# Moving denominators and a unit's last values up to the next unit's first logits in an attention kernel

## The chip, the cores and the metric

The kernel runs on one core of a Trainium2 chip. The metric is the device time of one execution in microseconds; the time before is the median of three runs, and a separate execution was taken by the hardware profiler. Engines are named as in the profile: PE is TensorE's matmul stream and PEld its weight loads, DVE is VectorE, ACT is ScalarE, POOL is GpSimd, SP is SyncE, whose queue issues the transfers.

## What is computed

Eight images of 512 channels by 32x32 pixels, all in float32, go through two layers. The part that matters here is the attention in the first layer, which is run twice for each image (`i` = 0, 1):

```python
def bot_attention(x, qkv_w, rw, rh):
    b, c, h, w = x.shape
    hw = h * w
    qkv = conv2d(x, qkv_w, 0).reshape(b, 3, HEADS, HD, hw)
    q, k, v = (qkv[:, 0], qkv[:, 1], qkv[:, 2])
    r = (rw + rh).reshape(1, HEADS, HD, hw)
    logits = jnp.einsum('bhdi,bhdj->bhij', q, k + r) * HD ** (-0.5)
    a = jax.nn.softmax(logits, axis=-1)
    out = jnp.einsum('bhij,bhdj->bhdi', a, v)
    return out.reshape(b, c, h, w)
...
t = cbs(x, cv1_w, cv1_bn, 0)
ys = [t[:, :C], t[:, C:]]
for i in range(N):
    yi = ys[-1]
    z = cbs(yi, m_cv1_w[i], m_cv1_bn[i], 1)
    z = bot_attention(z, m_qkv_w[i], m_rw[i], m_rh[i])
    z = jax.nn.silu(bn_eval(conv2d(z, m_cv2_w[i], 0), m_cv2_bn[i]))
    ys.append(yi + z)
return cbs(jnp.concatenate(ys, axis=1), cv2_w, cv2_bn, 0)
```

There are 4 heads of 64 channels (`HD`) over 1024 pixels. `cbs` is a convolution, a batch norm with fixed statistics and a silu; `cv1`, `cv2` and `m_cv2` are 1x1 convolutions and `m_cv1` is 3x3. A group norm precedes each layer, and the second layer is a 1x1 convolution with a masked weight. Both layers are added to their input.

## The kernel before

The attention is cut into 64 units. A unit is one image, one `i`, one pair of heads (`hp`) and one half of the 1024 queries (512 columns). Four units make a slot (one image and `i`), and there are 16 slots. The logits are kept transposed: keys lie on the partitions, in eight tiles (`KT` = 8), and queries lie along the columns.

The steps of a unit, with their lines and the names that the profile shows:

- `logits(t)` (L502, `lg`): one matmul for each of the two heads, on 64 rows of the array each, into a bank of PSUM each. ScalarE copies both to SBUF (L508, `st`), and VectorE keeps the running maximum over the tiles (L513, `mx`).
- `top` (L521, L522): TensorE transposes the maxima (`mt`, eight transposes in two banks), and VectorE reduces each bank to the negated maximum of each query (`nm`).
- `spread` (L529, `mb`): eight more transposes bring the negated maxima back along the columns.
- `soften(t)` (L533): VectorE adds `mb` to the logits of a tile; `exponent(t)` (L537) takes the exponent on ScalarE, and GpSimd adds the result to a running sum (L542, `sum`; `acc` in the code).
- `values(t)` (L548, `po`): two matmuls, one for each head, on 64 columns of the array each, accumulate the eight tiles in one PSUM tile `po`.
- `finish` (L560, L562): two matmuls with ones give the denominators (`den`), also on 64 columns each, and ScalarE copies them to `rb`. `divide(part)` (L567, L569) takes the reciprocal of half of `rb` and multiplies that half of `po` by it into `q`, on VectorE.

All other work of TensorE is filler between the units' steps: the 1x1 convolutions (L175: `cv`, `qk`, `l`, `m`), the 3x3 convolution in a transformed form (L305, `m`) and the products of `v` (L397). `slot_filler` lists it for each slot. `advance(share)` takes filler from this list until the given share of the slot is reached; `steps` is 40, ten for each unit, and `base` is ten times the unit's number in its slot. `Clock` keeps a planned time: `tick` moves it on and issues what has become due, such as the statistics of a group norm.

The order in the loop is written out by hand, and a scheduler may still exchange instructions that are close together. While unit `u` does its softmax, the logits of the next unit `nxt` are issued among its steps, two tiles at a time. `before` is the unit ahead of `u`. So around a change of unit the order before is: last logits of `u`, filler, `values(6)` and `values(7)` of `before`, transposes `mt` of `u`, filler, `mb`, filler, `den` of `before`, and then in the loop at t = 0 the softening of `u` and the first two logits of `nxt`.

`in_turn` and `act_turn` fix the order of the named VectorE and ScalarE instructions among themselves. The pools that matter: five PSUM banks (`ps_f`) shared by `lg`, `mt`, `den` and all filler; one buffer each for `mb` (two banks) and `po`; ten buffers `st`, of which a unit fills eight; one buffer each for `mx` and `acc`.

Of the kernel before, what the change touches and what calls it, by code (L numbers as in the profile page):

```python
# [32 lines left out]
KT = 8  # L33
# [6 lines left out]
def conv_preact_kernel(ctx: ExitStack, tc: tile.TileContext, x, cv1, cv2, mcv1, qkv, mcv2, bn, rw, rh, conv, s_in, t_in, out):  # L40
# [27 lines left out]
    def bank(name):  # L68
        return ps_f.tile([P, HALF], F32, tag="bank", name=name)

    def half_tile(name):
        return tp.tile([P, HALF], F32, tag="t", name=name)
# [413 lines left out]
    class Unit:  # L486
# [69 lines left out]
        def finish(self):  # L556

            den = bank(f"den_{self.name}")
            for h in range(2):
                nc.tensor.matmul(den[HD * h : HD * h + HD], ones[:, :HD], self.acc[:, h], start=True, stop=True)  # L560
            self.rb = half_tile(f"rb_{self.name}")
            nc.scalar.copy(self.rb, den)  # L562
            self.divide(0)

        def divide(self, part):
            r = ts(part, HALF // 2)
# [184 lines left out]
    clock = Clock()  # L751
# [140 lines left out]
    def slot_filler(s):  # L892

        prev = slots[s - 1] if s else (None, 0)
        nxt = slots[s + 1] if s + 1 < len(slots) else (None, 0)
        todo, needed = [], 0.0

        def add(us, g):
            nonlocal needed
            todo.append((us, g))  # L900
            needed += us

        im, i = nxt
        add(8.0, bg.take(8.0))
        if im and i == 1:
            add(7.0, im.conv_m2(0))
            add(0.0, call(im.transform, 1, 3.0, 1.0))
            add(9.0, bg.take(9.0))
        products = im.conv3(i) if im else iter(())
        if prev[1] == 1:  # L910
            if im:
                add(21.3, (us for _, us in zip(range(16), products)))
            add(7.0, prev[0].conv_m2(1))
            add(0.0, call(lambda: finishing(prev[0])))
        if im:
            add(10.7 if prev[1] == 1 else 32.0, products)
            add(7.0, bg.take(7.0))
        if im:
            add(21.0, im.project(i))
        if s + 2 < len(slots) and slots[s + 2][1] == 0:  # L920
            add(0.0, call(slots[s + 2][0].load_y))
            add(0.0, call(slots[s + 2][0].transform, 0, 8.0, 1.3))
        rest = SHARE - needed if im else 70.0
        if rest > 0:
            todo.append((rest, bg.take(rest, wait=True)))
        total = sum(c for c, _ in todo)
        return needed, total, todo
# [76 lines left out]
    before = None  # L1004
    for s in range(len(slots)):
        needed, total, todo = slot_filler(s)
        state = {"done": 0.0}

        def filler():
            for us, g in todo:  # L1010
                start = state["done"]
                for cost in g:
                    clock.tick(cost)
                    state["done"] += cost
                    yield

                state["done"] = max(state["done"], start + us)

        fill = filler()

        def advance(share):
            goal = max(share * total, min(1.0, share / 0.74) * needed + 0.1)
            while state["done"] < goal:
                if next(fill, "end") == "end":
                    break

        steps = 4 * (KT + 2)
        for j in range(4):
            u = units[4 * s + j]
            nxt = units[4 * s + j + 1] if 4 * s + j + 1 < len(units) else None  # L1030
            base = j * (KT + 2)
            u.top()
            clock.tick(0.9)
            advance((base + 1) / steps)
            u.spread()
            clock.tick(0.9)
            advance((base + 2) / steps)
            if before:
                before.finish()
                clock.tick(0.9)  # L1040
            for t in range(0, KT, 2):
                u.soften(t)
                if before and t == 0:
                    before.divide(1)
                u.soften(t + 1)
                if t:
                    u.exponent(t)
                    u.values(t - 2)
                    u.values(t - 1)
                    clock.tick(2.0)  # L1050
                if nxt:
                    nxt.logits(t)
                    nxt.logits(t + 1)
                    clock.tick(2.0)

                if not t:
                    u.exponent(t)
                u.exponent(t + 1)
                advance((base + 4 + t) / steps)
            u.values(KT - 2)  # L1060
            u.values(KT - 1)
            clock.tick(2.0)
            before = u
        for _ in fill:
            pass

    before.finish()
    before.divide(1)
    im = images[NB - 1]
    clock.run(bg.take(7.0, force=True))  # L1070
# [54 lines left out]
```

## Time and profile before

| what | value |
|---|---|
| median of the runs | 3250.11 us (3249.44 to 3253.17, three runs) |
| profiled execution, its own time | 3244.98 us |
| span of the profiled execution | 3243.3 us |
| granted TensorE clock | 0.994 |
| PE busy | 3141.8 us, 11668 records |
| DVE busy | 2071.7 us |
| ACT busy | 1727.1 us |
| POOL busy | 1243.3 us |
| DMA | 399.28 MB, mean 123 GB/s |

The span is from the first to the last instruction. Busy is the time in which at least one instruction of the engine was shown running; the ends of matmuls are modelled, so that a matmul's length in the list can reach into the next one, and the distance from start to start says how long the array was taken. A float32 matmul leaves two records, a transpose one. A wait in the lists is idle time of an engine just before an instruction, put down to what ended it last.

### The profile page before, as it was taken

How to read it: one execution, taken by the hardware profiler on the slowest of the kernel's cores; microseconds unless marked ns; L12 is line 12 of the kernel's file. 1: busy time of each engine (PE TensorE's matmuls, PEld its weight loads, DVE VectorE, ACT ScalarE, POOL GpSimd, SP SyncE). 2: the span in 40 equal slices, each digit the busy share in tenths (PEclk: the TensorE clock that was granted, in tenths of full speed). 3: DMA queues.
4: the chain of work that ended last, by engine and by line, in shares of the span. 5: the costliest groups of instructions: out<-in, count | busy, mean ns of one | idle time of the engine just before them, and what ended most of it. 6: DMA issues, size and time to landing. Idle time of an engine off the chain costs nothing.

```text
span 3243.3 us, 33195 instructions
## 1 busy us (share of the span) xinstructions
PE 3141.8 (97%) x11668; PEld 1519.6 (47%) x11668; DVE 2071.7 (64%) x2718; ACT 1727.1 (53%) x2353; POOL 1243.3 (38%) x971
## 2 busy tenths in 40 slices
PE   7999999999999999999999999999999999999999
PEld 3645444454445454454445454454445454453343
DVE  5446676667666576667666676667666676666642
ACT  3255765854655555544655455554645455555631
POOL 2113343445433444344434443345434443344420
PEclk9999999999999999999999999999999999999999
DMA  8841442421233232423233242423233241413366
GB/s 295 301 158 62 158 151 81 142 79 59 88 113 127 69 133 69 143 85 136 88 111 130 89 138 67 145 81 132 95 111 123 88 146 58 154 62 120 104 213 218
DMA packets 142006, 399.28 MB, mean 123 GB/s; under 512 B 13072, under 2 KB 14352, under 8 KB 141840
## 3 DMA queue, kind: packets, MB, share of 16 engines
q1 hardware_dynamic: 141120, 396.94, 36.4%
q8 instruction: 92, 1.51, 0.2%
q14 instruction: 74, 0.61, 0.1%
q10 hardware_dynamic: 720, 0.23, 0.0%
HBM read 317.42 MB, written 79.69 MB: 122 GB/s over the span
## 4 chain that ended last, share of the span: by engine, by line
PE 72%; DVE 11%; ACT 5%; DMA 4%; issue 3%; POOL 0%; SPq 0%; ACTq 0%; DVEq 0%
PE cv L175 14%; PE m L305 14%; PE po L548 12%; PE lg L502 11%; PE qk L175 6%; PE l L175 5%; PE v L397 3%; DVE st L533 2%; DVE rb L567 2%; PE mt L521 2%; PE den L560 2%; PE mb L529 2%; DVE mx L513 2%; PE m L175 1%; DMA x<-in_x 1%
## 5 line engine op out<-in xcount | busy, mean ns | idle before, releaser
L542 POOL TENSOR_TENSOR sum<-sum,st 128x512 f32<-128x512 f32 x768 | 993.8, 1319 | 719.2 <-ACT st L537 719.1
L537 ACT ACTIVATE st<-st 128x1024 f32<-128x1024 f32 x512 | 540.8, 1069 | 390.9 <-DVE st L533 389.8
L513 DVE TENSOR_TENSOR mx<-mx,lg 128x512 f32<-128x512 f32 x768 | 477.6, 682 | 370.2 <-ACT st L508 370.1
L533 DVE TENSOR_TENSOR st<-st,mb 128x1024 f32<-128x1024 f32 x512 | 604.9, 1214 | 71.3 <-PE mb L529 71.3
L508 ACT COPY st<-lg 128x512 f32<-128x512 f32 x1024 | 524.4, 596 | 228.0 <-PE lg L502 222.8
L305 PE MATMUL m<-plane,w_m 128*128 128x256 f32 x2304 | 530.7, 384 | 20.7 <-ACT cv2s L130 8.4
L502 PE MATMUL lg<-q,k 64*128 64x512 f32 x2048 | 534.1, 619 | 2.8 <-ACT y L130 1.4
L548 PE MATMUL po<-st,v 128*64 128x512 f32 x2048 | 514.2, 611 | 20.4 <-ACT st L537 12.6
L305 PEld LDWEIGHTS m<-plane,w_m 128*128 128x128 f32 x2304 | 427.5, 190 | 145.9 <-issue 44.8
L542 POOL TENSOR_TENSOR sum<-st,st 128x512 f32<-128x512 f32 x128 | 168.0, 1334 | 847.5 <-ACT st L537 807.2
L175 PE MATMUL cv<-y,w_cv 128*128 128x512 f32 x1024 | 466.6, 600 | 11.2 <-DVE mx L513 7.4
L502 PEld LDWEIGHTS lg<-q,k 64*128 64x128 f32 x2048 | 189.2, 186 | 337.6 <-issue 245.1
L175 PEld LDWEIGHTS cv<-y,w_cv 128*128 128x128 f32 x1024 | 185.3, 190 | 258.7 <-issue 234.3
L548 PEld LDWEIGHTS po<-st,v 128*64 128x64 f32 x2048 | 124.6, 137 | 335.8 <-issue 229.5
L567 DVE RECIPROCAL rb<-rb 128x256 f32<-128x256 f32 x128 | 215.2, 1723 | 61.5 <-ACT rb L562 61.5
L175 PE MATMUL l<-x,w_l 128*128 128x512 f32 x512 | 235.0, 603 | 8.3 <-DVE mx L513 7.7
L175 PE MATMUL cv<-x,w_cv 128*128 128x512 f32 x512 | 233.8, 603 | 8.6 <-ACT x L165 2.4
L175 PE MATMUL qk<-z,w_qkv 128*128 128x512 f32 x512 | 235.9, 604 | 3.7 <-DVE mx L513 3.7
L522 DVE TENSOR_REDUCE nm<-mt 128x4 f32<-128x512 f32 x128 | 83.3, 686 | 229.3 <-PE mt L521 229.0
L562 ACT COPY rb<-den 128x512 f32<-128x512 f32 x64 | 37.4, 584 | 233.7 <-PE den L560 233.3
L175 PEld LDWEIGHTS qk<-z,w_qkv 128*128 128x128 f32 x512 | 93.6, 191 | 130.8 <-issue 95.9
L175 PEld LDWEIGHTS l<-x,w_l 128*128 128x128 f32 x512 | 92.7, 190 | 131.2 <-issue 106.1
(145 smaller groups left out, 2445.5 us busy)
## 6 DMA issues: line engine op xcount, KB each, us to landing
w_m<-w_m SPq DMA_DIRECT2D x96, 768.0 KB, 4.4
w_cv<-in_cv SPq DMA_DIRECT2D x90, 512.0 KB, 3.5
y<-y SPq DMA_DIRECT2D x64, 512.0 KB, 4.8
x<-in_x SPq DMA_DIRECT2D x56, 512.0 KB, 5.4
y<-y SPq DMA_DIRECT2D x64, 256.0 KB, 3.5
k<-r SPq DMA_DIRECT2D x32, 512.0 KB, 3.8
res<-y SPq DMA_DIRECT2D x32, 512.0 KB, 4.2
xr<-in_x SPq DMA_DIRECT2D x32, 512.0 KB, 4.2
```

What stands on the lines that cost most here:

```text
L175: nc.tensor.matmul(ps, w, moving, start=(n == 0), stop=(n == len(terms) - 1))
L305: nc.tensor.matmul(ps[:, ts(co, 256)].rearrange("p (t x) -> p t x", x=F), w[:, co, c, dx], u[:, 9 * c : 9 * c + 8, dx : dx + F], start=(j ...
L397: nc.tensor.matmul(ps[:, ts(j, P)], z[:, c, ts(4 * j4 + j, P)], w[:, c, 512 + P * hp : 512 + P * hp + P], start=(c == 0), stop=(c == IT - 1),)
L502: nc.tensor.matmul(lg[h], self.k[r, ts(t, P)], self.q[r, self.hp, ts(self.half, HALF)], start=True, stop=True)
L508: act_turn(nc.scalar.copy(st[:, h], lg[h]))
L513: in_turn(nc.vector.tensor_tensor(self.mx[:, h], so_far[:, h], lg[h], ALU.max))
L522: nc.vector.tensor_reduce(self.nm[:, h], mt, AX.X, ALU.max, negate=True)
L533: in_turn(nc.vector.tensor_tensor(st, st, flat(self.mb), ALU.add))
L537: act_turn(nc.scalar.activation(st, st, AF.Exp))
L542: nc.gpsimd.tensor_tensor(self.acc[:, h], so_far[:, h], self.st[t][:, h], ALU.add)
L548: nc.tensor.matmul(self.po[HD * h : HD * h + HD], self.v[:, t, ts(h, HD)], self.st[t][:, h], start=(t == 0), stop=(t == KT - 1),)
L567: nc.vector.reciprocal(self.rb[:, r], self.rb[:, r])
```

## The change

`finish` no longer calls `divide(0)`. In the loop, `finish` of the unit before moves behind the filler to t = 0, and directly behind its matmuls and the first two softenings come the unit's last two values, then both parts of the division, then the next unit's first two logits. The last values are no longer issued at the end of the loop over `t`. The filler ahead of `top`, between `top` and `spread`, and behind `spread` is dealt out up to shares 0.7, 1.4 and 2 (none ahead of `top`, then up to 1 and up to 2 in the kernel before). At the end of the program the last unit's values and both parts of its division follow its `finish`.

```diff
             self.rb = half_tile(f"rb_{self.name}")
             nc.scalar.copy(self.rb, den)
-            self.divide(0)
...
             base = j * (KT + 2)
+
+            advance((base + 0.7) / steps)
             u.top()
             clock.tick(0.9)
-            advance((base + 1) / steps)
+            advance((base + 1.4) / steps)
             u.spread()
             clock.tick(0.9)
             advance((base + 2) / steps)
-            if before:
-                before.finish()
-                clock.tick(0.9)
             for t in range(0, KT, 2):
+                if before and t == 0:
+                    before.finish()
+                    clock.tick(0.9)
                 u.soften(t)
-                if before and t == 0:
-                    before.divide(1)
                 u.soften(t + 1)
                 if t:
                     u.exponent(t)
-                    u.values(t - 2)
-                    u.values(t - 1)
+
+                lag = u if t else before
+                if lag:
+                    lag.values((t - 2) % KT)
+                    lag.values((t - 1) % KT)
                     clock.tick(2.0)
+                if before and t == 0:
+                    before.divide(0)
+                    before.divide(1)
                 if nxt:
                     nxt.logits(t)
                     nxt.logits(t + 1)
...
                 advance((base + 4 + t) / steps)
-            u.values(KT - 2)
-            u.values(KT - 1)
-            clock.tick(2.0)
             before = u
         for _ in fill:
             pass
 
     before.finish()
+    before.values(KT - 2)
+    before.values(KT - 1)
+    before.divide(0)
     before.divide(1)
```

## The prediction

> **What bounds the kernel now.** I read the page's first part, then busy time by stretches, then TensorE's waits in the main stretch, then TensorE's timeline around a change of unit. PE is busy 97% of the span and DVE, the next, 64%:
>
> ```profile
> PE 3141.8 (97%) x11668; PEld 1519.6 (47%) x11668; DVE 2071.7 (64%) x2718; ACT 1727.1 (53%) x2353; POOL 1243.3 (38%) x971
> ...
> 213.00:3100.00 2887.00, 2813.92 (x10744) 1359.02 (x10746) 1932.07 (x2467) 1632.19 (x2223) 1196.20 (x925) 0.99 0.33 108
> ```
>
> The second line is the stretch in which attention units follow each other: PE works 2813.9 of 2887.0 us, so 73.1 us are waits. The waits of PE (who waited, for whom, total us, times, longest) add up to just that; those that the change touches are
>
> ```profile
> PE po L548 <- ACT st L537: 12.6, 12, 2.9
> PE cv L175 <- DVE mx L513: 9.7, 8, 2.1
> ...
> PE po L548 <- DVE q L569: 7.6, 8, 2.5
> ...
> PE mt L521 <- DVE mx L513: 2.7, 4, 0.8
> PE mb L529 <- DVE nm L522: 1.9, 2, 1.1
> ```
>
> So TensorE's own stream sets the time; waits can give back 2.2% at the very most. But the stream has a second price, seen only from start to start. One change of unit (start, length, engine, line, operation), then pieces of others:
>
> ```profile
> 1576.45 5.42 PE L175 MATMUL cv<-y,w_cv 128*128 128x512 f32 x12
> 1581.80 1.94 PE L548 MATMUL po<-st,v 128*64 128x512 f32 x8
> 1583.67 1.09 PE L521 MATMUL mt<-ident,mx 128*128 128x128 f32 x8
> 1584.60 3.60 PE L175 MATMUL cv<-y,w_cv 128*128 128x512 f32 x8
> 1588.03 1.04 PE L529 MATMUL mb<-ident,nm 128*128 128x128 f32 x8
> 1588.90 1.88 PE L175 MATMUL cv<-y,w_cv 128*128 128x512 f32 x4
> 1590.72 1.08 PE L560 MATMUL den<-sum,ones 128*64 128x512 f32 x4
> 1591.73 1.99 PE L502 MATMUL lg<-q,k 64*128 64x512 f32 x8
> ...
> 1680.46 1.04 PE L521 MATMUL mt<-ident,mx 128*128 128x128 f32 x8
> 1681.33 3.60 PE L175 MATMUL cv<-y,w_cv 128*128 128x512 f32 x8
> ...
> 1685.64 3.60 PE L175 MATMUL cv<-y,w_cv 128*128 128x512 f32 x8
> 1689.17 1.08 PE L560 MATMUL den<-sum,ones 128*64 128x512 f32 x4
> ...
> 3098.74 3.65 PE L548 MATMUL po<-st,v 128*64 128x512 f32 x16
> 3102.33 1.98 PE L175 MATMUL l<-x,w_l 128*128 128x512 f32 x4
> ```
>
> There are three shapes of array: whole (128\*128: cv, m, qk, v, l, mt, mb), half columns (128\*64: po, den) and half rows (64\*128: lg). Eight cv between mt and mb, whole on both sides, take 1588.03 - 1584.60 = 3.43 us; eight that end at den take 1689.17 - 1685.64 = 3.53: leaving the whole shape costs 0.10. mt takes 0.93 after po (1583.67 to 1584.60) and 0.87 after cv (1680.46 to 1681.33): coming back costs 0.06. Twelve cv between lg and po take 5.35 where 12 x 0.429 is 5.15: 0.20 for that way out and in. A run of po costs 1.87 for 8 records (1581.80 to 1583.67) but 3.59 for 16 (3098.74 to 3102.33), so 1.72 for each eight and 0.15 for the run. lg costs 1.92 for 8, so 0.20 for the run.
>
> **What the Trainium skill says.** "TensorEngine Tiling (Array Packing)", section Tiling Modes, says that changing the tiling mode, not merely the tile, drains TensorE. The trace agrees and prices it: 0.10 to 0.20 us a change, above. "TensorE: Matmul & The Clock Gate", Part 2, says that matmuls keep program order and only weight loads are pulled ahead; so whatever waits holds all behind it, as the equality of the summed waits with the 73 us confirms. "Perfetto Trace Analysis", Identifying the Most-Contended Engine, warns that matmul busy time says little because matmuls are pipelined; hence starts, not lengths, here.
>
> **The change, part by part.** TensorE's instruction lists of both kernels are fixed when they are built, and I counted shapes in them; the list of before has 963 changes of shape, and the trace has 963.
>
> 1. *The last values (four po matmuls, 8 records) go from ahead of mt to just behind den.* po and den have one shape. At the boundary above, whole-po-mt and whole-den-lg become whole-den-po-lg: saved 0.10 + 0.15 + 0.06 = 0.31 us. Over the whole list the changes of shape fall from 963 to 818: half-column runs 351 to 278 (73 x 0.15 = 11.0 us), half-row runs 273 to 262 (11 x 0.20 = 2.2), whole-array runs behind a half-column run 93 to 30 (63 x 0.16 = 10.1), whole-array runs behind lg 246 to 248 (2 x 0.20 = 0.4 lost). A matmul of these shapes that stands alone lasts as long as a pair side by side (den alone: 1.00 us, from 2005.26 to 2006.27; both: 1.01). Pairs and lone ones come to 592 before and 594 after for po and den (lone dens, one half ahead of mb, rise from 8 boundaries to 15, lone po's fall), and 523 and 518 for lg: 3 x 0.86 = 2.6 saved. **Sum: 25.5 us off TensorE's stream**, which nothing covers.
>
> 2. *Waits at the boundary that lose their cause.* The eight waits of po for q (7.6 us): po has one PSUM buffer, so a unit's first values wait for the previous unit's division. That division still starts from den, while po and lg, 3.6 us, now lie between, not lg alone: gone. Of the waits of po for st L537, seven are at the last two values (0.8, 0.8, 0.4, 1.2, 2.9, 0.4, 1.2 = 7.7 us): these values come some 8 us later now (1.9 + mt 0.9 + 1.7 + mb 0.9 + 1.4 + den 1.0): gone. The waits of mt for mx (2.7): in front of mt, po's 1.87 us give way to filler of about as much, and no boundary has less than 1.8 us of work there where the least was 0.9: gone. Sum 18.0 us.
>
> 3. *Filler shares 1 and 2 become 0.7, 1.4 and 2.* No work is added. But between mt and mb the mean work falls from 2.5 to 1.7 us, and 15 boundaries have only one den half (1.0 us) there, 8 before. nm's second reduction ends 1.98 us after mt's start on an idle DVE; mb then starts 2.03 after it. An st or conv operation of DVE in between (up to 1.2 us) now shows as a wait of mb, behind which den, po and lg queue. The trace of before does not show this wait at such a distance. Bounds: 0, if DVE is idle as it was in the eight such boundaries of before; 63 x 0.7 = 44 us if each lost microsecond were waited for. I take 1.2 us at a third of the 15 (6.0) and 0.1 at each of the other 48 (4.8), about 11 us, near the lower end, since DVE stands idle ahead of nm at 60 of 128 reductions (229 us in all).
>
> 4. *The division behind the values.* Reciprocals (1.73 us each) and products (0.41) stand in DVE's list where they stood: behind the first two softenings, ahead of the next unit's first maximum. Cost 0. Its product now needs po, which ends 1.9 us after den; the reciprocals end over 4 us after den, and cover that. Should they not, the first maximum and with it two lg banks would be late.
>
> 5. *What is passed.* lg's first copies (L508) go into the buffers of the values just moved; these precede lg on PE, so cost 0. Everything from lg on (copies, first exp, first po) shifts together. SP's and POOL's lists keep their work, a few neighbours exchanged: 0. ACT's table loads fall from 228 to 222, 7.7 us off an engine that is not on the path.
>
> Sum: -25.5 - 18.0 + 11 = **-32.5 us**, against the profiled execution's 3245.0 (span 3243.3). The median of the runs, 3250.1, is 5.1 above it; I take the difference from the median: **3217.6 us**.
>
> **Rivals.**
> - *Cover of nm too thin* (chance 0.22): the wait of part 3 eats all that part 2 frees, and more: 25 us of it, 0.4 a boundary. 3250.1 - 25.5 - 18 + 25 = 3231.6. For: DVE's st follows mb at once and its queue is full in some boundaries. Against: DVE's idle time before nm.
> - *More waits fall* (0.11): DVE gets po's 1.87 us more between mb and the middle of the unit, so the waits of cv for mx (9.7) and of l, m and qk for it (15.1) shrink by half, and part 3 costs nothing: 3250.1 - 25.5 - 18 - 12 = 3194.6.
> - *Regrouping is worth nothing* (0.04): den and po drain between them anyhow. Then parts 2 and 3 alone remain, 3250.1 - 18 + 11 = 3243, at the edge of what can be told from no change. Against: po directly followed by den, near 3113, costs about 0.1 less than two runs.
> - *Slower* (0.03): POOL's last sums (2.5 us behind the last exp) hold den, and behind den now po and lg. TensorE reaches den about 1.75 us sooner than before. The last sum leads den by at least 1.4 us now, under 3 at only two of 63 boundaries. It decides above (25.5 + 7 + 6.5) / 63 = 0.6 us a boundary; at 0.7, 44 us, the time is 3250.1 - 32.5 + 44 = 3261.6.
> - That the order is not as the diff says is ruled out by the lists.
>
> **Numbers.** The main case has 0.60 and spans 3205 to 3228 by itself. The range 3198 to 3237 adds most of the thin-cover case and the near half of the good one. About 0.2% (6.5 us) is what a measurement of this kernel can tell from no change: faster 0.92, within 0.05, slower 0.03.
>
> **What would show it.** Right: PE's busy time near 3116; den and po adjacent, about 2.73 us from den's start to lg's; no wait of po for q; no wait of mt for mx. Part 3: a line of mb waiting for nm of about 11 us. Wrong: PE's busy time unchanged; den waiting for sum L542; PE's waits above 90 us.

## The result and the profile after

The changed kernel takes 3200.7 us (median; 3195.75 to 3204.39), against 3250.11 before: a ratio of 0.9845, 95% interval 0.9833 to 0.9857, so about 49 us faster. The profiled execution took 3202.9 us, its span is 3201.1; the profiled execution of before took 3245.0, its span 3243.3. These two lie 42.2 us apart, and the account below is made on them.

The page's first part and busy time by stretches, the stretch of the attention units being the second line (PE busy, then PEld, DVE, ACT, POOL):

```profile
PE 3115.6 (97%) x11668; PEld 1527.5 (48%) x11668; DVE 2076.9 (65%) x2718; ACT 1718.5 (54%) x2347; POOL 1244.7 (39%) x971
...
213.00:3055.00 2842.00, 2782.91 (x10736) 1364.64 (x10734) 1932.87 (x2462) 1620.31 (x2214) 1196.45 (x924) 0.99 0.32 109
```

PE is busy 26.2 us less (3141.8 to 3115.6), and what is left of the span, PE's idle time, is 16.0 us less (101.5 to 85.5). Together they are the 42.2. How much of that is stream and how much waiting is less firm than the sum: a second profile of the same program (f1 below) has a span of 3201.4 us, but PE busy for 3106.6 and idle for 94.8, at a granted clock of 0.997 instead of 0.993. Among the units the waits fell from 73.1 to 59.1 us (66.9 in the second profile). PE's waits in that stretch, those that answer to the lines of before:

```profile
PE po L548 <- ACT st L537: 18.2, 16, 2.9
...
PE cv L175 <- DVE mx L513: 6.6, 7, 2.1
...
PE mb L529 <- DVE nm L522: 1.0, 1, 1.0
```

po no longer waits for q, nor mt for mx: neither line is there, in the second profile either. mb waits for nm once (twice in the second profile). The wait of po for the exponents has grown, from 12.6 to 18.2.

TensorE's timeline at the boundary that was shown of before (start, length, engine, line, operation):

```profile
1562.48 1.04 PE L521 MATMUL mt<-ident,mx 128*128 128x128 f32 x8
1563.36 1.88 PE L175 MATMUL cv<-y,w_cv 128*128 128x512 f32 x4
1565.08 1.04 PE L529 MATMUL mb<-ident,nm 128*128 128x128 f32 x8
1565.95 1.88 PE L175 MATMUL cv<-y,w_cv 128*128 128x512 f32 x4
1567.76 1.08 PE L560 MATMUL den<-sum,ones 128*64 128x512 f32 x4
1568.67 1.89 PE L548 MATMUL po<-st,v 128*64 128x512 f32 x8
1570.49 1.99 PE L502 MATMUL lg<-q,k 64*128 64x512 f32 x8
```

mt now stands between whole-array work and takes 0.88 us (1562.48 to 1563.36) where it took 0.93. From den to lg there pass 2.73 us (1567.76 to 1570.49); apart, the two runs took 1.01 + 1.87 = 2.88.

### The profile page after: what moved, and what is told of

Its sections match the earlier page's. It is cut to its first block, busy times and chain, and to the rows that moved or that the text cites. A ratio compares the mean times of both kernels' runs of the same rounds, so it can differ in the third digit from the quotient of the medians.

```text
span 3201.1 us, 33271 instructions
## 1 busy us (share of the span) xinstructions
PE 3115.6 (97%) x11668; PEld 1527.5 (48%) x11668; DVE 2076.9 (65%) x2718; ACT 1718.5 (54%) x2347; POOL 1244.7 (39%) x971
## 4 chain that ended last, share of the span: by engine, by line
PE 71%; DVE 7%; ACT 4%; DMA 2%; issue 2%; POOL 0%; SPq 0%; ACTq 0%; DVEq 0%
PE m L305 14%; PE cv L175 13%; PE po L548 11%; PE lg L502 11%; PE l L175 6%; PE qk L175 6%; PE v L397 3%; PE den L560 2%; PE m L175 2%; DVE st L533 2%; PE mb L529 2%; PE mt L521 2%; ACT st L508 1%; DVE mx L513 1%; ACT st L537 1%
## 5 line engine op out<-in xcount | busy, mean ns | idle before, releaser
L548 PE MATMUL po<-st,v 128*64 128x512 f32 x2048 | 516.6, 607 | 18.3 <-ACT st L537 18.2
L502 PE MATMUL lg<-q,k 64*128 64x512 f32 x2048 | 522.4, 617 | 2.3 <-ACT y L130 1.7
L502 PEld LDWEIGHTS lg<-q,k 64*128 64x128 f32 x2048 | 180.8, 186 | 333.5 <-issue 264.3
L548 PEld LDWEIGHTS po<-st,v 128*64 128x64 f32 x2048 | 131.9, 137 | 328.4 <-issue 238.1
L175 PEld LDWEIGHTS cv<-x,w_cv 128*128 128x128 f32 x512 | 95.0, 193 | 128.1 <-issue 107.9
```

What stands on the lines that cost most here:

```text
L175: nc.tensor.matmul(ps, w, moving, start=(n == 0), stop=(n == len(terms) - 1))
L502: nc.tensor.matmul(lg[h], self.k[r, ts(t, P)], self.q[r, self.hp, ts(self.half, HALF)], start=True, stop=True)
L548: nc.tensor.matmul(self.po[HD * h : HD * h + HD], self.v[:, t, ts(h, HD)], self.st[t][:, h], start=(t == 0), stop=(t == KT - 1),)
```

## Experiments

"Shape price" below is the sum of the prediction's first step, made again with the same prices for the kernel's own instruction list; it is 25.4 us less than before for the changed kernel. It counts matmuls that stand alone too, not only changes of shape. Since PE's busy time also holds the time lost to a lower granted clock, one column takes (1 - granted clock) x span off it. That is an estimate: the clock is given to three digits, which leaves about 3 us open in a difference, and the two profiles of the changed kernel come out 4 us apart. Both are differences to before, in us; ratios are of the times, with 95% intervals.

| kernel | changes of shape | shape price | PE busy, clock taken off | ratio |
|---|---|---|---|---|
| changed kernel | 818 | -25.4 | -29.1 | 0.9845 (0.9833 to 0.9857) |
| the same again, f1 | 818 | -25.4 | -25.3 | 0.9858 (0.9843 to 0.9872) |
| e1, old shares | 813 | -28.9 | -25.1 | 0.988 (0.9863 to 0.9897) |
| e2, new shares only | 998 | +14.4 | +23.1 | 1.0044 (1.0029 to 1.0059) |
| e3, values apart from den | 899 | -12.0 | -7.1 | 0.9934 (0.9921 to 0.9947) |
| e4, filler to 0.80 | 797 | -38.9 | -41.1 | 0.9822 (0.9807 to 0.9836) |
| f2, thin cover | 818 | -25.4 | -22.7 | 0.9891 (0.9876 to 0.9907) |
| f3, thick cover | 818 | -25.4 | -24.7 | 0.9884 (0.9867 to 0.9901) |
| f4, 0.80 and cover | 796 | -40.1 | -40.3 | 0.9829 (0.9814 to 0.9844) |
| g1, shares 0.4, 1.1 | 818 | -25.4 | -19.6 | 0.990 (0.988 to 0.992) |
| g2, shares 0.6, 1.3 | 818 | -25.4 | -25.0 | 0.9855 (0.9832 to 0.9877) |
| g3, shares 0.8, 1.5 | 818 | -25.4 | -29.1 | 0.9853 (0.9832 to 0.9874) |

The experiments ask how much of the changed kernel's 49 us is stream, how much is waits, and which edit brings them. Theory at the start: the regrouping of array shapes is the larger part, lost waits the smaller, and the shares of filler do nothing. Rival: the waits and the shares are the gain.

**e1: the changed kernel with the shares of before.**

```diff
-            advance((base + 0.7) / steps)
             u.top()
...
-            advance((base + 1.4) / steps)
+            advance((base + 1) / steps)
```

> The changed kernel with the filler shares of the kernel before (none ahead of the transposes, then 1 and 2). Theory: the gain comes from where the last values stand, next to the denominators, and not from the shares. The instruction list has 813 changes of array shape (changed kernel 818, before 963) and eight boundaries with a lone den half ahead of mb instead of 15; at the prices read from the trace of before that is 3.5 us less of TensorE's own time than in the changed kernel. Expected within 8 us of the changed kernel, about 3197, PE busy about 3112; waits of po for q gone here too. Rival: the shares carry the lost waits (mt for mx among them); then it stands 10 us or more above the changed kernel, over 3210, and mt waits for mx.

It took 3218.6 us beside 3256.0 of before. The rival's number came: 37 us faster than before, not 50. The wait of mt for mx is back, five times, and mb waits four times for nm (PE's waits, whole execution):

```profile
PE mt L521 <- DVE mx L513: 4.3, 5, 1.5
...
PE mb L529 <- DVE nm L522: 2.2, 4, 1.0
```

The stream is as cheap as in f1 (-25.1 and -25.3 in the table), so the filler shares do carry a part, some 7 to 12 us by the two comparisons of the changed kernel, and the theory's "nothing" fell. That it comes through waits fits the traces: PE's idle time and the time lost to the clock, taken together, are 118.1 us here, 107.9 in the changed kernel and 104.4 in f1. The two lines above are 6.5 us of it; the two profiles of the changed kernel have 1.0 and 2.0 there.

**e2: the kernel before with the new shares.**

```diff
+            advance((base + 0.7) / steps)
             u.top()
...
-            advance((base + 1) / steps)
+            advance((base + 1.4) / steps)
```

> The kernel before with the new filler shares alone (0.7, 1.4, 2); values and denominators stay where they were. Theory: no gain, rather a loss: the list has 998 changes of array shape (before 963), about 14 us more of TensorE's time, against 3 us of waits of mt for mx. Expected 3255 to 3268, PE busy about 3155, and po still waits for q, about 8 us. Rival: filler ahead of the transposes is itself worth the waits, so 5 to 15 us below before, 3235 to 3245.

3270.4 us, 14.4 slower than before: the theory's direction. That the loss is the shape price to the tenth is chance, since PE's busy time rose by 23 us in the profile, to 3165.0 where about 3155 was expected, and its idle time fell by 4. po waits 3.5 us for q here, less than the 8 expected. So the shares alone lose, and together with the move they gain (e1 beside the changed kernel). One reason is on the lists: alone they add 35 changes of shape, behind the move 5 (813 to 818), by the shape price 14.4 us and 3.5. That the values which were moved had covered the maxima ahead of mt fits e1's waits, but was not tried by itself.

**e3: the last values behind mb, not next to den.**

```diff
             u.spread()
             clock.tick(0.9)
+            if before:
+                before.values(KT - 2)
+                before.values(KT - 1)
+                clock.tick(2.0)
             advance((base + 2) / steps)
...
-                lag = u if t else before
-                if lag:
-                    lag.values((t - 2) % KT)
-                    lag.values((t - 1) % KT)
+                if t:
+                    u.values(t - 2)
+                    u.values(t - 1)
                     clock.tick(2.0)
```

> The changed kernel with the last values right behind mb, with filler between them and den wherever the list has some: late as in the change, but in most boundaries not next to den. 899 changes of array shape; at the prices of before 13.4 us more of TensorE's own time than in the changed kernel. Theory (regrouping is the larger part, the later place of the values the smaller): about 3214, PE busy about 3129, waits of PE like those of the changed kernel, po not waiting for q. Rival (all of the gain is waits that are lost because the values come later, and the shapes cost nothing): the same as the changed kernel, about 3201, PE busy unchanged at 3116.

3234.5 us, 21.5 faster than before and so some 25 to 28 slower than the changed kernel (49 and 46 faster in its two comparisons). The rival fell: PE's busy time rose to 3131.4, where the theory had 3129. But the loss is twice what the theory had, and one line of PE's waits shows a reason:

```profile
PE po L548 <- DVE q L568: 11.0, 11, 1.9
```

Here lg follows den at once, as before the change, and po waits for the division again. In the changed kernel, where po stands between den and lg, this line is not there; po's waits for exponents and for q together are 18.2 us there, 19.0 in f1 and 23.6 here.

**e4: the needed filler dealt out to 0.80 of the slot.**

```diff
-            goal = max(share * total, min(1.0, share / 0.74) * needed + 0.1)
+            goal = max(share * total, min(1.0, share / 0.80) * needed + 0.1)
```

> The changed kernel with the needed filler of a slot dealt out up to 0.80 of the slot instead of 0.74, so that less often no filler lies between mt and mb. 797 changes of array shape, six lone den halves instead of 15; at the prices of before 13.5 us less of TensorE's own time. Theory (TensorE's stream sets the time, and each change of shape is paid): about 3188, PE busy about 3102. Rival: the next image's q and k come later, and its first logits or the denominators wait for them; then PE's waits grow by what the shapes save, and the time stays at 3201 or above.

0.9822, 7.5 to 12 us below the changed kernel's two ratios. The stream fell as priced (PE 3103.6, expected 3102). The waits moved, though not to q and k as the rival had it: the 3x3 filler waits for mx, 18.4 us in all, against 2.0 in the changed kernel, while po's waits for exponents fell from 18.2 to 8.6. All idle time of PE is 90.6 us, between the changed kernel's two profiles (85.5 and 94.8), so that waits gave some of the price back is not shown.

**f1, f2, f3: the changed kernel again, and thinner and thicker cover of nm.** f2 and f3 are the prediction's third step by itself.

```diff
-            advance((base + 1.4) / steps)
+            advance((base + 1.0) / steps)   # f2
+            advance((base + 2.0) / steps)   # f3
```

> The changed kernel itself, beside the next three on one chip. Both theories: 0.982 to 0.987 of the kernel before.

> The changed kernel with the share behind the transposes cut from 1.4 to 1.0, so that on average 1.1 us of TensorE's work lies between mt and mb instead of 1.8, and 40 of 63 boundaries have only about 1 us there (15 in the changed kernel). Changes of array shape stay at 818. Theory of the prediction's third step (cover of nm is what a boundary can run short of): mb waits for nm, 12 to 20 us in all, and the time rises by about as much. Rival (VectorE is idle when the transposes end, nm is ready 2 us after they start, and 1 us of work is cover enough): mb waits under 4 us, time within 6 us of the changed kernel.

> The changed kernel with the share behind the transposes raised from 1.4 to 2.0: all filler of the boundary stands between mt and mb (2.9 us on average), none between mb and den. Changes of array shape stay at 818. If thin cover costs something beyond the 1.0 us of waits of mb that the trace shows, this is faster than the changed kernel by up to 10 us. Rival (cover is no issue): within 6 us of it; should it be slower, then because the softening starts about 1 us later and the first exponents reach po late.

f1 took 3202.2 us, f2 3212.5, f3 3211.8, beside 3248.7 of before. In f2 mb waits

```profile
PE mb L529 <- DVE nm L522: 3.7, 4, 1.9
```

which is the rival's "under 4", with 40 boundaries of about 1 us of cover; yet the time rose by 10 us, which the rival excluded. In f3 no wait of mb is left and the time rose by 10 us too. So neither account is right: a boundary does not pay for thin cover by itself, and both directions cost. I followed the two traces unit by unit against f1. f2 loses 4.7 us up to the first unit of the fifth slot, 5.3 after the last unit's first logits, and the other 6.6 in a few steps; f3 loses 3.2 up to the fifth slot and the rest likewise. Between the steps whole slots pass without a loss, so it is no price for each boundary. The largest steps lie where these traces show TensorE's clock at half and f1's does not: f2's clock is at half from 747.1 to 757.3 us, f1's from 746.6 to 750.0. By (1 - granted clock) x span, an estimate, f2 lost 25.7 us to the clock, f3 22.5 and f1 9.6; f2's profile is 16.6 us longer than f1's and f3's 7.3, and neither has more idle time of PE. The granted clock is on record for the other executions too: it averages 0.9950 for f1, 0.9938 for f2 and 0.9925 for f3, which is worth about 4 of f2's 10 us and 8 of f3's. Why the clock is lower in these two, and where f2's other 6 us lie, stays open. f3's own reason, first exponents that reach po late, does not show: that wait is 15.9 us, and 19.0 in f1.

**f4: 0.80 with the share 1.7.**

```diff
-            goal = max(share * total, min(1.0, share / 0.74) * needed + 0.1)
+            goal = max(share * total, min(1.0, share / 0.80) * needed + 0.1)
...
-            advance((base + 1.4) / steps)
+            advance((base + 1.7) / steps)
```

> The changed kernel with the needed filler dealt out up to 0.80 of the slot and the share behind the transposes at 1.7. 796 changes of array shape, 14.7 us less of TensorE's own time than in the changed kernel at the prices of before. Theory: faster than the changed kernel by 7 to 15 us, about 3190 to 3198 where the kernel before takes 3256, since the waits of filler for mx that grew when filler was dealt out to 0.80 take some of it. Rival: these waits take all of it; no faster than the changed kernel.

3194.4 us (3191.7 to 3195.2) beside f1's 3202.2 (3201.1 to 3207.3) on the same chip: 7.8 us faster, a version that beats both kernels. PE's stream is 15 us cheaper, as priced, and the time fell by about half of that. The 3x3 filler again waits for mx,

```profile
PE m L305 <- DVE mx L513: 19.7, 7, 3.2
```

against 2.1 us in f1, but po's waits for exponents fell from 19.0 to 6.1, and PE's idle time as a whole is 88.8 us against f1's 94.8. So these waits do not account for the missing half, which stays open.

**g1, g2, g3: more or less filler ahead of mt, the same between mt and mb.** e1 had left open whether each boundary pays for missing filler ahead of mt, or single pieces of filler decide.

```diff
-            advance((base + 0.7) / steps)
+            advance((base + 0.4) / steps)   # g1; g2: 0.6, g3: 0.8
...
-            advance((base + 1.4) / steps)
+            advance((base + 1.1) / steps)   # g1; g2: 1.3, g3: 1.5
```

> The changed kernel with the shares 0.4 and 1.1 in place of 0.7 and 1.4: the same filler between mt and mb, less of it ahead of mt. 818 changes of array shape, as in the changed kernel, so the same stream. Theory A (filler ahead of mt takes the place of the values that stood there, and each boundary pays for what is missing): between none (about 0.989 of before) and 0.7 (0.985), about 0.987, mt waiting for mx up to 3 us. Theory B (where single pieces of filler fall decides, not a price for each boundary): anywhere within 10 us of the changed kernel, without order in the share.

> The same with shares 0.6 and 1.3, 818 changes of array shape. Theory A: within 3 us of the changed kernel, about 0.986 of before. Theory B: anywhere within 10 us of the changed kernel.

> The same with shares 0.8 and 1.5, 818 changes of array shape. Theory A: no slower than the changed kernel, about 0.985 of before. Theory B: anywhere within 10 us of it, slower more likely than faster, since two other settings around it were 10 us slower.

With 0, 0.4, 0.6, 0.7 and 0.8 the ratios are 0.988, 0.990, 0.9855, 0.9845 (0.9858 again) and 0.9853: a step between 0.4 and 0.6 and level beyond it. In the traces mx's last instruction ends later than mt's first transpose starts in 11, 7, 2 and 0 of 63 boundaries with 0, 0.4, 0.6 and 0.7. That is theory A's order, but not its numbers: at 0.990 instead of the expected 0.987, 0.4 of a share is worth no more than none. Nor is it mt that waits in g1's list but mb, five times, behind transposes and reductions that came late:

```profile
PE mb L529 <- DVE nm L522: 5.2, 5, 1.5
```

In g2 that wait is 2.0 us, so it names 3 of the 13 us between g1 and g2; PE's idle time as a whole is 9.1 us longer in g1's profile. Theory B allowed 10 us and any order; g1 lies about 13 above g2 and g3, and the order is that of the share, so for the filler ahead of mt it fell.

## Why the prediction was right, and where its terms were off

It forecast 32.5 us and a time of 3217.6; the time, 3200.7, lies in the range, and the sign and the main mechanism, the regrouping, hold. The gain was half as large again as forecast, and the time lies below the 3205 to 3228 that the main case spanned by itself. That the sum came out as near as it did is in part luck: step 2 promised about 13 us too much and step 3 took off about 12 too much. By its steps:

1. *The regrouping, 25.5 us.* Measured: 26.2 on the two profiles, 35.2 with f1's; with the clock taken off, 29.1 and 25.3. Over the twelve rows of the table PE's busy time without the clock's part follows the shape price within 6 us, but for e2, 8.7 above. den to lg came out at the 2.73 us expected. This step is shown: e3 undoes the neighbourhood in most boundaries, and its busy time rises, by 18 to 22 us with the clock taken off where the list says 13.4; e4 and f4 go the other way as priced.
2. *Lost waits, 18.0 us.* Of the three lines of this step, 22.9 us, 18.2 stayed, so they gave 4.7. po for q, 7.6: gone, and back in e3. mt for mx, 2.7: gone, and back in e1. The 7.7 us of po for the exponents were wrong. The line rose instead, by 5.6. Three of the seven waits stayed, 6.9 us, since in those boundaries the scheduler left the first pair of the two last values where it had been, ahead of mt; this is one of them:

```profile
1337.75 1.97 PE L548 MATMUL po<-st,v 128*64 128x512 f32 x2 [2.85 <-ACT st L537]
1339.65 6.19 PE L305 MATMUL m<-plane,w_m 128*128 128x256 f32 x18
...
1347.20 1.04 PE L521 MATMUL mt<-ident,mx 128*128 128x128 f32 x8
```

   And ten new waits came at a unit's first values, 6.9 us in all, where q had cost 7.6, so that there hardly anything was won. Nine of them lie in the boundaries with little filler, where lg starts 5.71 us after mt where it had started after 4.04 to 4.62, the exponents come later with it, and at most four records of filler lie between, as here:

```profile
1445.53 1.99 PE L502 MATMUL lg<-q,k 64*128 64x512 f32 x8
1447.45 1.98 PE L175 MATMUL l<-x,w_l 128*128 128x512 f32 x4
1449.80 2.02 PE L548 MATMUL po<-st,v 128*64 128x512 f32 x8 [0.37 <-ACT st L537]
```

   My "everything from lg on shifts together" was right, but at these boundaries that chain, and no longer q, is what po waits for.
3. *Thin cover of nm, +11 us.* This term was nothing: the wait went from 1.9 to 1.0 us (2.0 in f1). The reductions end 1.92 or 1.93 us after mt's start in 54 of the 64 units, and one den half is enough cover. f2 shows that even at 40 thin boundaries it is 3.7 us. The 10 us that f2 loses are not in this wait.
4. *The division behind the values, 0.* DVE's order hardly changed, and no wait names it. Right.
5. *What is passed, 0.* Right for the queues, but not for the exponents, as step 2 says. No wait of lg for st, none of den for sum: the slower rival did not appear.

What the sum missed beside the terms: the waits of cv, l, m and qk for mx fell from 24.8 to 19.2 us, and of the 3x3 filler for z from 6.0 to 2.6. That is the rival "more waits fall", which held in part; in f1 the first of these is 22.6. The remaining 7 us between the profiles' 42 and the medians' 49 arise because the profiled execution of before lies 5.1 below the median of its kernel's runs and that of the changed kernel 2.2 above.

No step of the sum names the granted clock, and it went along with the gain. Over the 27 executions of the kernel before that stand beside e1 to g3 it averages 0.9914, over the changed kernel's nine 0.9946. By (1 - granted clock) x span that is about 28 and 17 us, so some 11 of the 49 us. As an estimate, then, 25 to 29 us of the gain are stream, some 11 went with the clock, and about 10 are waits. Why the clock is higher stays open: waits of 1.9 us or more are not clearly fewer (13 among the units before, 11 and 15 in the two profiles of the changed kernel). The profiled execution of before, at 0.994, hides this.

One reading of the prediction shows less than it says: PE's summed waits equal its idle time because the list puts all idle time down to some wait, so the equality does not confirm that matmuls keep their order.

## What to carry to other kernels

When TensorE is the bottleneck, list its instructions by array shape and price each change of shape from start to start: runs of the same shape that can be joined are time that no other engine can hide. Work that stood ahead of a dependent step was also its cover; when it is moved, something must take its place, and here how much was a step and not a slope (0.4 of a share was too little, 0.6 enough). Between the matmuls that start a division and those that wait for its result, put matmuls that need neither, and look for the next wait that may take the old one's place.

## What the runs showed of the hardware

Two matmuls of 64 columns run side by side even if they belong to different products. Where den's second half stood alone behind mb, the first po started 0.01 us after it:

```profile
1442.81 0.64 PE L560 MATMUL den<-sum,ones 128*64 128x512 f32 x1
1442.82 0.64 PE L548 MATMUL po<-st,v 128*64 128x512 f32 x1
1443.29 0.59 PE L560 MATMUL den<-sum,ones 128*64 128x512 f32 x1
1443.30 2.30 PE L548 MATMUL po<-st,v 128*64 128x512 f32 x7
```

This does not make the split free. From here to lg at 1445.53 there are five matmuls of 64 columns in 2.72 us, as long as six take elsewhere (2.73): den's half has a partner, but the last of the four po then stands alone.

Long waits and a lower granted clock go together here. TensorE's granted clock fell to half for 3.4 us or a multiple of it, 13.7 at most, in 7 to 13 places of each of the thirteen traces. From 213 to 3055 us they have 98 such places, and 91 begin during a wait of PE of 1.9 us or more or within 3.5 us of its end. Of the 158 such waits 91 have one. Around the wait of 2.52 us that ends at 743.60 us the clock reads (columns: stretch, its length, PE busy, granted clock, DMA share, GB/s)

```profile
740.00:745.00 5.00, 2.48 (x10) 0.81 0.01 3
745.00:750.00 5.00, 5.00 (x11) 0.51 0.00 0
```

This fits with one and the same program showing PE busy for 3115.6 us at a clock of 0.993 and 3106.6 at 0.997 in spans of 3201.1 and 3201.4 us, though no run changed the clock or such a wait by itself, so that a long wait is paid for twice is argued and not shown. PE's busy time of two profiles should be compared with the clock beside it.
